# A second block of picked columns on TensorE in each octet of a graph layer

## The chip, the core and the metric

The kernel runs on one core of one Trainium2 chip. Its time is the device time of one execution; of three executions before the change the median is 3237.42 us (3233.37 to 3243.10). Times are in microseconds (us) unless another unit stands beside them. The engines are named as in the profile: PE is TensorE (PEld its weight loads), DVE is VectorE, ACT is ScalarE, POOL is GpSimd, and SP is SyncE, which here only issues transfers.

## The reference

One layer of a graph network over 12500 nodes with 64 features and 400000 edges, sorted by destination, all in float32:

```python
m_in = concatenate([x[src], x[dst], edge_attr])       # 64 + 64 + 16 features an edge
h = silu(m_in @ W1 + b1)                              # first layer, 64 wide
messages = silu(h @ W2 + b2)                          # second layer, 64 wide
agg = segment_sum(messages, dst, num_segments=12500)
y = silu(concatenate([x, agg]) @ W3 + b3)
out = layernorm(x + y)
```

The kernel's main difficulty is `x[src]`: the sources are random, so each of the 400000 edges wants a row (or, transposed, a column) of 64 floats from some place.

## The kernel before

The edges are cut into tiles of 128, and eight tiles are an **octet**; there are 391 octets, and one loop over `o` (the loop over `NO + 2`) writes out the work of all engines, software-pipelined: while octet `o` is in its first layer, octet `o - 2` is in its second and the messages of octet `o - 4` are added up. Two tiles that are computed side by side, one on the upper and one on the lower 64 partitions, are a **pair**; an octet has four.

What a source's node contributes to an edge can come to the first layer in several ways, and the work is split over them:

- GpSimd gathers a tile's 128 rows with one indirect DMA (`gather`, line 504). Early octets read the node features; from octet 12 on they read the table `pa`, which holds the features already multiplied by their part of W1. TensorE then transposes these rows (line 606).
- ScalarE copies single columns out of `xs` and `x2`, which hold all nodes' features transposed on chip; one activation serves two edges of a pair (`columns`, line 414). The column's address is a register, loaded in batches (line 397).
- VectorE does the same with a byte-wise maximum (line 416), also two edges at a time.
- SyncE issues one small DMA a row (`rows`, line 444).
- TensorE **picks** (`pick`, line 370): it loads the identity as weights and streams a single column of `xs`, so that the column lands in PSUM. A pick is one matmul in the code and two in the records. Sixteen addresses at a time are loaded into registers ahead of them (line 363).

A pair that one of the last four has filled is not gathered. Picked columns collect in the upper part of the two PSUM banks `pg`, whose lower part takes the sums of line 637. Odd octets use one bank, even ones the other. When both banks have a page of 128 columns, `place` lets VectorE copy it into `px` (line 381), and the first layer multiplies it like any other pair (line 609). `filled`, `whole`, `pairs`, `slots` and `counts` work out which octet takes a finished pair.

How much each of them does in an octet is set by constants: `ACOLS` (48 columns ahead of the first activation of an octet and 32 ahead of the second on ScalarE; in one octet of four it is 16 fewer), `VCOLS` with `VRATE` (32 columns at two or three places on VectorE), `PCOLS` (picks of TensorE), and `ROWS` (rows of SyncE, as a fraction).

On each engine the instructions run in the order in which the loop writes them; there is no scheduler for TensorE, ScalarE, VectorE and SyncE. In an octet TensorE's order is:

1. `turn` (line 571): transposes of the one-hot rows of the next octet, which VectorE then copies out (line 581); the buffer is single, so line 571 waits for that copy;
2. `window_product` (line 528);
3. `first_layer` (lines 606, 609, 610), whose result ScalarE activates at line 613;
4. `pick` (lines 363 and 370);
5. `add_up` (line 637);
6. `second_layer` (lines 622 and 624), whose result ScalarE activates at line 628; that buffer is single too, so line 622 waits for ScalarE;
7. in about half of the octets one product for the nodes' own layer: `node_x` (line 680) or `node_sums` (line 686).

## Time and profile before

| | before |
|---|---|
| median of 3 executions | 3237.42 us |
| profiled execution | 3241.3 us |
| its span, first to last instruction | 3239.4 us |
| mean granted TensorE clock | 0.836 |
| TensorE busy | 2713.9 us, 84% |
| ScalarE busy | 3076.0 us, 95% |
| VectorE busy | 2052.1 us, 63% |
| GpSimd busy | 2428.7 us, 75% |

Busy time leaves out the instructions that load registers and those that issue transfers; an engine can be occupied where this table calls it idle, and the idle time before a group ("issue" where nothing else is seen to hold it up) has to be read with it. The durations of matmuls overlap, so a group's busy time is not its count times its mean. The granted clock is TensorE's, as a share of full speed.

### The profile page before, as it was taken

To read this page: it belongs to the slowest core of one execution; us is meant where nothing else is said; L and a number is where in the kernel's file an instruction comes from. 1 tells how busy PE (TensorE), PEld (TensorE's weight loads), DVE (VectorE), ACT (ScalarE), POOL (GpSimd) and SP (SyncE) were. 2 spreads that over 40 slices of the span, in tenths; PEclk is the share of its full clock that TensorE was granted. 3 is DMA by queue.
4 is the path that set the end of the run, shared out by engine and by line. 5 is a ranking of instruction groups with operands and counts; after the bars stand their busy time and mean duration, and the time that the engine had idled before them with its cause. 6 is when DMAs were issued, how large, how long until landed. Compare 5 with 4: busy or idle time off the path is not lost. (4 is left out here: it accounts for less than half of the span.)

```text
span 3239.4 us, 111913 instructions
## 1 busy us (share of the span) xinstructions
PE 2713.9 (84%) x27140; PEld 2268.4 (70%) x27140; DVE 2052.1 (63%) x18157; ACT 3076.0 (95%) x15178; POOL 2428.7 (75%) x2567
## 2 busy tenths in 40 slices
PE   6888888889888888888888888888888888888865
PEld 4677767767777777776776776777776767777654
DVE  4466666666666666666666666666666666666663
ACT  1599999999999999999999999999999999999993
POOL 7777777777777777777777777777777777777775
PEclk7788888888788888788888888887888888788888
DMA  7222222222222222221222222222222222222121
GB/s 143 53 41 41 45 41 41 43 43 41 44 48 44 44 43 41 44 43 39 50 46 39 45 43 39 45 43 44 49 41 41 43 43 43 41 48 46 41 41 38
DMA packets 158957, 148.18 MB, mean 46 GB/s; under 512 B 102367, under 2 KB 112357, under 8 KB 157525
## 3 DMA queue, kind: packets, MB, share of 16 engines
q0 software_dynamic: 81888, 84.02, 14.6%
q1 hardware_dynamic: 61902, 47.16, 5.7%
q10 hardware_dynamic: 14502, 9.75, 1.4%
q8 instruction: 221, 3.62, 0.5%
q14 instruction: 444, 3.63, 0.4%
HBM read 134.30 MB, written 6.40 MB: 43 GB/s over the span
## 5 line engine op out<-in xcount | busy, mean ns | idle before, releaser
L504 POOL DMA_INDIRECT ga<-pa,sc x2463 | 2336.6, 949 | 756.8 <-issue 659.9
L414 ACT ACTIVATE cx<-xs,x 128x1 f32 x14336 | 2805.5, 382 | 9.8 <-issue 4.8
L416 DVE TENSOR_TENSOR cx<-xs,x 128x4 uint8 x15744 | 1271.9, 154 | 1043.4 <-issue 1027.3
L370 PEld LDWEIGHTS pg<-xs,ident 128*64 128x64 f32 x11776 | 770.6, 146 | 363.2 <-issue 310.3
L370 PE MATMUL pg<-xs,ident 128*64 x11776 | 801.6, 202 | 32.5 <-DVE px L381 31.8
L624 PEld LDWEIGHTS p<-w2d,h 128*128 128x128 f32 x3126 | 537.1, 243 | 244.4 <-issue 224.8
L624 PE MATMUL p<-w2d,h 128*128 128x128 f32 x3126 | 539.7, 330 | 0.0
L610 PE MATMUL p<-oh,xw 128*128 128x512 f32 (+1 forms) x758 | 454.6, 686 | 0.0
L622 PE MATMUL p<-b2r,one 128*128 128x512 bf16 x391 | 177.7, 454 | 229.3 <-ACT m L628 228.3
L571 PE MATMUL ph<-identb,eh 128*96 128x128 bf16 x1563 | 195.6, 261 | 169.3 <-DVE oh L581 165.5
L637 PE MATMUL pg<-eh,m 128*64 128x48 f32 x6250 | 320.4, 236 | 1.4 <-ACT m L628 1.4
L613 ACT ACTIVATE h<-p 128x512 f32<-128x512 f32 x391 | 263.4, 674 | 50.5 <-PE p L610 25.7
L628 ACT ACTIVATE m<-p 128x512 f32<-128x512 f32 x391 | 263.5, 674 | 36.2 <-PE p L624 34.5
L571 PEld LDWEIGHTS <-eh 128*96 128x96 bf16 x1563 | 153.9, 154 | 198.3 <-DVE oh L581 191.3
L606 PE MATMUL p<-ident,ga 128*128 128x128 f32 x1232 | 249.8, 319 | 45.8 <-DMA ga<-pa,sc 45.6
L637 PEld LDWEIGHTS pg<-eh,m 128*64 128x64 f32 x6250 | 269.9, 148 | 18.1 <-issue 15.1
L581 DVE COPY oh<-ph 96x512 f32<-96x512 f32 x391 | 263.1, 673 | 1.2 <-PE ph L571 1.2
L606 PEld LDWEIGHTS p<-ident,ga 128*128 128x128 f32 x1232 | 189.6, 171 | 54.7 <-issue 48.3
L553 DVE TENSOR_TENSOR eh<-wrow,dc 128x384 f32<-128x384 f32 x392 | 213.0, 544 | 17.8 <-ACT z L692 8.7
L528 PE MATMUL mm<-w1bb,xr 66*96 66x128 f32 x782 | 201.3, 347 | 8.4 <-DMA xr<-in_xt 8.3
L610 PEld LDWEIGHTS p<-oh,xw 128*128 128x128 f32 x758 | 139.3, 229 | 0.0
L528 PEld LDWEIGHTS mm<-w1bb,xr 66*96 66x96 f32 x782 | 127.1, 210 | 9.7 <-DMA xr<-in_xt 5.8
(115 smaller groups left out, 1194.0 us busy)
## 6 DMA issues: line engine op xcount, KB each, us to landing
rx<-pa SPq DMA_DIRECT2D x6400, 0.2 KB
ga<-pa,sc POOLq DMA_INDIRECT x2463
oh<-in_attr SPq DMA_DIRECT2D x130, 192.0 KB
xr<-in_xt SPq DMA_DIRECT2D x391, 24.4 KB
cxi<-in_src_pair SPq DMA_DIRECT2D x235, 1.0 KB
xs<-in_xt ACTq DMA_DIRECT2D x6, 512.0 KB
pa<-v ACTq DMA_DIRECT2D x12, 256.0 KB
x<-in_xt ACTq DMA_DIRECT2D x6, 512.0 KB
```

Of the source, the lines that this page charges most:

```text
L370: nc.tensor.matmul(g[:, s, k:k + 1], ident[:, :D], xs.bitcast(U8)[:, ds(at, 4)].bitcast(F32), start=True, stop=True, skip_group_check=True)
L414: nc.scalar.activation(cols[key][:, k:k + 1], word(i, xb, XADDR), AF.Identity, bias=word(i + 4, x2b, X2ADDR))
L416: nc.vector.tensor_tensor(t[:, 4 * k:4 * k + 4], at(i, xb, XADDR), at(i + 4, x2b, X2ADDR), op=OP.max)
L504: nc.gpsimd.indirect_dma_start(out=ga[:, i, :], out_offset=None, in_=x if o < RAW else pa[:, :], in_offset=bass.IndirectOffsetOnAxis(ap=sc ...
L528: nc.tensor.matmul(pw[:E, :], winrow[o], w1bb.rearrange("k s m -> k (s m)"), start=True, stop=True)
L571: nc.tensor.matmul(ph[:E, i, :], eh[:, i, :, 1], identb, start=(i == 0), stop=(i == k - 1), skip_group_check=True)
L606: nc.tensor.matmul(p1[:, i, :], g2.rearrange("p s d -> p (s d)"), ident, is_transpose=True, start=(i == c), stop=False, skip_group_check=True)
L610: nc.tensor.matmul(p1[:, :k], xw[o % 3], oh, start=False, stop=True, skip_group_check=True)
L613: nc.scalar.activation(h[:, :k], p1[:, :k], AF.Silu)
L624: nc.tensor.matmul(p2[:, 2 * i:2 * i + 2, :].rearrange("p s d -> p (s d)"), h[:, i, :], w2d, start=False, stop=(i == k - 1), skip_group_ch ...
L628: nc.scalar.activation(m[:, :n2], p2[:, :n2], AF.Silu)
L637: nc.tensor.matmul(pg[s * D:(s + 1) * D, :], m[:, i, :], eh[:, i // 2, :, s], start=(i < 2), stop=(i >= n - 2), skip_group_check=True)
```

## The change

Four constants change, and `pick` is called twice in an octet, each time for 16 columns: once where it stood, behind the first layer, and once behind the second layer (`behind()` writes `add_up` and `second_layer`), ahead of the product for the nodes. A page of 128 columns in each bank is then full after 8 octets instead of 16. ScalarE takes the smaller number of columns in one octet of three instead of one of four (74.7 columns an octet on average instead of 76), VectorE 81.6 instead of 83.2, SyncE 16.8 rows instead of 17.1; what is left goes to GpSimd's gathers, of which there are 36 fewer.

```diff
-PCOLS = 16
-ROWS = (256, 15)
-VRATE = (26, 10)
+PCOLS = 32
+ROWS = (1024, 61)
+VRATE = (51, 20)
...
             if eng == ENG.Activation:
-                return ACOLS if (o - BEGIN) % 4 < 3 else (ACOLS[0] - 16, ACOLS[1])
+                return ACOLS if (o - BEGIN) % 3 < 2 else (ACOLS[0] - 16, ACOLS[1])
...
-        def pick(o):
+        def pick(o, lo, up):
             if o < BEGIN:
                 return
-            c, hi, b = filled(o, o % 2), filled(o + 1, o % 2), o % 2
+            b = o % 2
+            c, hi = filled(o, b) + lo, filled(o, b) + up
             while c < hi:
...
                 if o < NO:
                     first_layer(o)
-                pick(o)
+                pick(o, 0, PCOLS // 2)
...
                 if o != NO - 1:
                     behind()
+                pick(o, PCOLS // 2, PCOLS)
                 for f, a in todo.get(o, []) if o < NO else []:
                     if f in (node_begin, node_x, node_sums):
                         f(*a)
```

`pick` is one line longer, so the lines behind its head stand one lower in the changed kernel (line 370 becomes 371, 637 becomes 638).

## The prediction

> **What bounds the kernel now.** I read the page's engine table and costliest groups first, then the waits, then the granted clock, and last TensorE's timeline beside the clock. Units are us; a group's columns are busy time, mean ns of one, and idle time before it.

> ```profile
> PE 2713.9 (84%) x27140; PEld 2268.4 (70%) x27140; DVE 2052.1 (63%) x18157; ACT 3076.0 (95%) x15178; POOL 2428.7 (75%) x2567
> ...
> L504 POOL DMA_INDIRECT ga<-pa,sc x2463 | 2336.6, 949 | 756.8 <-issue 659.9
> L414 ACT ACTIVATE cx<-xs,x 128x1 f32 x14336 | 2805.5, 382 | 9.8 <-issue 4.8
> L416 DVE TENSOR_TENSOR cx<-xs,x 128x4 uint8 x15744 | 1271.9, 154 | 1043.4 <-issue 1027.3
> L370 PE MATMUL pg<-xs,ident 128*64 x11776 | 801.6, 202 | 32.5 <-DVE px L381 31.8
> ```

> From the full list of groups, the gathers of the start:

> ```profile
> L504 POOL DMA_INDIRECT ga<-in_x,sc x96 | 91.2, 950 | 31.6 <-issue 27.1 <-DMA ga<-in_x,sc 2.3 <-DMA sc<-in_src_c 1.3
> ```

> GpSimd is the bound: 2336.6 busy plus 756.8 of gap, nearly all "issue", is 3093.4 for 2463 gathers, 1.256 each; with the 96 gathers of the start, 91.2 and 31.6, it fills 3216 of the 3239.4 span. ScalarE stands at 95%. VectorE's 2052 plus 1027 of register loading before its columns is 3079, also 95%. TensorE alone has room, 525 idle, and the waits say on whom:

> ```profile
> PE p L622 <- ACT m L628: 228.3, 167, 3.3
> PE ph L571 <- DVE oh L581: 165.5, 121, 5.3
> PE p L606 <- DMA ga<-pa,sc: 45.6, 36, 3.8
> PE pg L370 <- DVE px L381: 31.8, 17, 3.2
> ```

> It waits for VectorE and ScalarE far more than for gathers: it is early nearly everywhere. The granted clock of the run:

> ```profile
> core 0: 3239.4 us, clock 0.836
> ```

> ```profile
> 2402.82 0.66 PE L571 MATMUL ph<-identb,eh 128*96 128x128 bf16 x4 [1.59 <-DVE oh L581]
> ...
> 2406.45 3.47 PE L370 MATMUL pg<-xs,ident 128*64 x31
> 2409.68 0.34 PE L637 MATMUL pg<-eh,m 128*64 128x48 f32 x1
> ...
> 2413.00 0.63 PE L571 MATMUL ph<-identb,eh 128*96 128x128 bf16 x4
> ...
> 2416.12 1.97 PE L370 MATMUL pg<-xs,ident 128*64 x31
> 2417.90 0.26 PE L637 MATMUL pg<-eh,m 128*64 128x48 f32 x1
> ...
> 2419.70 0.39 PE L571 MATMUL ph<-identb,eh 128*96 128x128 bf16 x4
> ...
> 2421.68 1.97 PE L370 MATMUL pg<-xs,ident 128*64 x31
> ```

> A cold octet (half clock, no wait inside) takes 2413.00 - 2402.82 = 10.18, a warm one 2421.68 - 2416.12 = 5.56. Sixteen picks take 2417.90 - 2416.12 = 1.78 and one record more, say 1.85, warm, and 3.23 and one more, say 3.3, cold.

> What sets the clock? It changes only on a grid of 3.413. I laid that grid over the trace and asked for TensorE's busy time in each step, first of all lines (length, PE busy, weight loads, DVE, ACT, POOL, granted clock), then of the picks alone (length, PE busy, weight loads, clock):

> ```profile
> 807.90:811.31 3.41, 3.41 (x56) 3.20 (x56) 2.08 (x18) 3.41 (x19) 2.50 (x4) 1.00 0.32 78
> 811.31:814.72 3.41, 3.41 (x38) 2.65 (x36) 1.76 (x23) 3.41 (x18) 2.50 (x4) 1.00 0.23 43
> ...
> 828.38:831.79 3.41, 2.65 (x49) 2.50 (x49) 1.97 (x24) 3.41 (x19) 2.69 (x3) 1.00 0.19 37
> 831.79:835.20 3.41, 1.72 (x8) 1.62 (x8) 1.90 (x19) 3.41 (x19) 2.59 (x3) 0.50 0.50 126
> ```

> ```profile
> 807.90:811.31 3.41, 2.03 (x32) 1.94 (x32) 1.00 0.32 78
> ...
> 828.38:831.79 3.41, 2.03 (x32) 1.94 (x32) 1.00 0.19 37
> ```

> ```profile
> 2405.34:2408.75 3.41, 3.41 (x24) 2.30 (x22) 1.94 (x20) 3.41 (x19) 2.52 (x3) 0.50 0.20 37
> 2408.75:2412.16 3.41, 3.41 (x34) 3.23 (x35) 2.15 (x20) 3.41 (x19) 2.50 (x4) 0.50 0.13 25
> 2412.16:2415.58 3.42, 3.42 (x16) 2.93 (x16) 1.85 (x18) 3.15 (x17) 2.54 (x3) 0.50 0.19 32
> 2415.58:2418.99 3.41, 3.41 (x53) 2.79 (x52) 2.24 (x21) 3.41 (x20) 2.76 (x3) 1.00 0.37 94
> ```

> ```profile
> 2405.34:2408.75 3.41, 2.29 (x22) 2.30 (x22) 0.50 0.20 37
> 2408.75:2412.16 3.41, 1.28 (x12) 1.19 (x12) 0.50 0.13 25
> 2412.16:2415.58 3.42, 0.00 (x0) 0.00 (x0) 0.50 0.19 32
> ```

> Subtract the picks. Warm, the step with 3.41 - 2.03 = 1.38 of other matmuls stayed warm; the one with 2.65 - 2.03 = 0.62 was followed by half speed, though TensorE was busy for 78% of it. Cold, 3.41 - 2.29 = 1.12 and 3.41 - 1.28 = 2.13 of other matmuls stayed cold with TensorE busy throughout; 3.42 of them brought full speed back. So a pick, a matmul that streams one column, counts for next to nothing. **Staying warm needs other matmuls for a share between 18% and 40% of a step, getting warm again a share between 62% and 100%.** Counting over the whole trace only the time in which columns stream, the lines that part best lie at 0.38 (12 of 632 warm steps on the wrong side) and about three quarters (9 of 309 cold ones).

> **The change, part by part.** Off GpSimd: 36 gathers (2463 to 2427 at line 504, now 505) by 1.256 = 45. Off ScalarE: 256 activations (14336 to 14080) by 2805.5/14336 = 0.196 = 50. Off VectorE: 384 operations by (1271.9 + 1027.3)/15744 = 0.146 = 56, less what twice the pages ask of it, 96 more copies at 0.215 and 24 more address operations at 0.297, together 28, so 28 net:

> ```profile
> L381 DVE COPY px<-pg 64x64 f32<-64x64 f32 x92 | 19.7, 215 | 1.4
> L486 DVE TENSOR_SCALAR pxi<-pxi 1x256 int32<-1x256 int32 x23 | 6.8, 297 | 0.3
> ```

> Sync issues 256 fewer rows and 24 more index loads, less work in all. Each has less to do, so if nothing else happened the profiled 3241.3 (its span, and 1.9 around it) would become 3241.3 - 45 = 3196.

> On TensorE: 6144 columns more, in 376 octets that now hold two blocks of 16 instead of one. Warm that is 376 x 1.85 = 696, cold 376 x 3.3 = 1241. Each block also loads its 16 addresses into registers:

> ```profile
> PEld pg L370 <- issue: 310.3, 346, 1.5
> ```

> The new load lies under lines 623 and 625, which hide it as line 610 does now; where TensorE has just waited at 623 it may show, by at most these 310.3/346 = 0.9, and only where TensorE was early. I take nothing. The page's 2713.9 busy plus even 696 is 3410, over the 3196: it fits only if the other work runs warmer than now. Per octet with the matmuls for the nodes:

> ```profile
> L686 PE MATMUL wrow<-w3s,agg 128*128 128x64 f32 x192 | 53.9, 373 | 0.6 <-DVE eh L553 0.6
> L680 PE MATMUL wrow<-w3x,xs 128*128 128x64 f32 x192 | 53.7, 372 | 0.0
> ```

> those add 107.6/391 = 0.28. Warm: 5.56 + 0.28 + 1.85 = 7.7. Cold: 10.18 + 0.28 + 3.3 = 13.8. The picks run from 102.0 to 3083.1 in 368 octets, 8.10 each:

> ```profile
> L370 PE MATMUL pg<-xs,ident x11776: 188/197/268, 102.0 to 3083.1; 128*64 x200
> ```

> With h the share of time at half speed, TensorE completes (1 - h)/7.7 + h/13.8 octets per us, and keeps up with 8.0 per octet (8.10 less 45/376) only for h under 0.09, a granted clock over 0.95.

> Where the new block stands decides h. TensorE, an octet without node products, from its first layer on; before:

> ```order
> L610 MATMUL p_121171<-oh,xw_178 128x512
> L363 TENSOR_LOAD pxi
> L370 MATMUL pg_238<-xs,ident 64x1 x16
> L637 MATMUL pg_238<-eh,m 64x48 x8
> L622 LDWEIGHTS one_120
> L622 MATMUL p_121404<-b2r,one_120 128x512
> L624 MATMUL p_121404<-w2d,h 128x128 x4
> L571 LDWEIGHTS eh
> ```

> and now (line numbers one higher):

> ```order
> L611 MATMUL p_112481<-oh,xw_170 128x512
> L364 TENSOR_LOAD pxi
> L371 MATMUL pg_237<-xs,ident 64x1 x16
> L638 MATMUL pg_237<-eh,m 64x48 x8
> L623 LDWEIGHTS one_120
> L623 MATMUL p_112752<-b2r,one_120 128x512
> L625 MATMUL p_112752<-w2d,h 128x128 x4
> L364 TENSOR_LOAD pxi
> L371 MATMUL pg_237<-xs,ident 64x1 x16
> L572 LDWEIGHTS eh
> ```

> The unbroken run from line 637 over 571 to 610 is cut in two. In an octet with a node product, TensorE's second block is followed by it:

> ```order
> L623 MATMUL p_118788<-b2r,one_120 128x512
> L625 MATMUL p_118788<-w2d,h 128x128 x4
> L364 TENSOR_LOAD pxi
> L371 MATMUL pg_237<-xs,ident 64x1 x16
> L687 MATMUL wrow<-w3s,agg 128x64
> L572 LDWEIGHTS eh
> ```

> Before, that product stood among other matmuls; now it lengthens a block that hardly streams.

> *Cold.* Now a run of 10.18 - 3.3 = 6.9 of counting work stands between blocks, so some step lies wholly inside it. After: 3.3 (lines 638 to 625, 2409.73 to 2413.00) and 3.6 (572 to 611, 2402.82 to 2406.45) between blocks of 3.3. A step of 3.41 holds three quarters, 2.55, of a run at 3.3 + 3.41 - 5.1 = 1.6 of its 3.41 offsets, or at 1.9 for the longer run. The runs start 6.6 apart, 1.94 steps, and the octet of 13.8 is 4.04 steps: the same offset comes back, and one that misses goes on missing. I take 0.57 to warm within the octet, after 0.6 of one on average; the other 0.43 drift by some 0.2 per octet through a band of 1.5, on average 3.6 octets. Mean cold stay: 0.57 x 0.6 + 0.43 x 4.1 = 2.1 octets.

> *Warm.* A step that holds a whole block keeps 40%, just over 0.38. A node product of some 0.4, mostly weight load, or any wait of over 0.1 beside a block takes it under. About 190 of 391 octets have such a product, and I put such a step at 4 in 10 of them; the waits at lines 622 and 571, and those for page copies, of which there are now twice as many, stand beside blocks too. I take 3 octets for a warm stay, with 2 and 9 as ends.

> Sum: (3 x 7.7 + 2.1 x 13.8)/5.1 = 10.2 per octet. 102 before the first pick + 376 x 10.2 + the tail of 3239.4 - 3083.1 less 8 octets of 8.1 = 92 + 1.9 around the span = **4030**. The other engines' 45 to 56 then vanish in waiting for TensorE. Ends: 9 warm to 1.4 cold give 8.5 and 3390; 2 warm to 4 cold give 11.8 and 4630; its own range is 3600 to 4500. The profiled run lies 0.1% over the median of 3237.42.

> **The rivals.** *TensorE gets warmer and GpSimd stays the bound: 3196, faster.* For it: 525 idle is filled, and idle is what sends the clock down now. Against it: a step busy for 78% fell, and picks fill idle time without counting. It decides at a clock of 0.95. [...]

> *The share of half speed stays 33%:* 1/(0.67/7.7 + 0.33/13.8) = 9.0, so 102 + 376 x 9.0 + 92 + 2 = 3580, slower. New blocks lose warmth and filled waits gain it; nothing in the rows makes them cancel exactly.

> *TensorE hardly ever gets warm again:* 13.8 throughout, 102 + 376 x 13.8 + 94 = 5385. The offset that comes back speaks for it; the 0.2 to 0.4 by which node products and the number of transposes shift an octet, against it.

> **How the numbers follow.** Forecast, 3600 to 4500: 0.62. The share unchanged or somewhat lower, 3260 to 3600: 0.18. GpSimd's bound: 0.12. Hardly ever warm: 0.05. Nothing to tell: 0.03. A difference under 0.3% is about what a measurement of this kernel can tell from none (its runs spread by that). So faster 0.12, same 0.03, slower 0.85. For 8 in 10 the range reaches down into the second case and leaves out the fast one and the top: 3260 to 4500.

> **What would show it.** Right: a granted clock well under 0.836, TensorE near 100% busy, the waits at lines 623 and 572 gone, ScalarE and VectorE waiting for lines 611 and 625, GpSimd for its buffers; steps filled by blocks and one run stay at 0.50. Wrong: a clock over 0.95, or warm steps whose other matmuls fill under a third. If only the price is off, the stays of 3 and 2.1 octets are what to measure.

## The result, and the profile after

The change makes the kernel slower by 45%: 4712.66 us median of 4 executions (4671.9 to 4767.75) against 3236.94 (3233.37 to 3243.1), ratio 1.4509 with a 95% interval of 1.4402 to 1.4616. The profiled execution took 4746.7, 0.7% over its median. The ratio is one of means: it leaves out the two executions of the change that lie over 1.5% above its fastest (4746.7, the profiled one, and 4767.75) and counts two that are not in the median (4731.97 and 4707.12). All times are us.

From the page of the changed kernel, the engine table, the first gathers, and the picks; then its waits and its clock:

```profile
PE 4693.4 (99%) x39447; PEld 3987.6 (84%) x39447; DVE 2077.6 (44%) x17887; ACT 3165.0 (67%) x14922; POOL 2389.0 (50%) x2531
...
L505 POOL DMA_INDIRECT ga<-pa,sc x2427 | 2297.2, 947 | 2301.5 <-PE p L607 1549.9
...
L371 PE MATMUL pg<-xs,ident 128*64 x24064 | 2267.5, 228 | 0.4 <-issue 0.4
```

```profile
POOL ga L505 <- PE p L607: 1549.9, 300, 12.5
...
DVE agg L649 <- PE pg L371: 1019.5, 238, 14.0
...
ACT m L629 <- PE p L625: 573.5, 244, 2.8
ACT h L614 <- PE p L611: 568.0, 263, 4.1
```

```profile
core 0: 4744.9 us, clock 0.614
```

The roles are exchanged. TensorE is busy 99% of the time and hardly waits for anybody (40 in all); GpSimd, which waited 6.4 for that line before, stands 1550 for gather buffers that line 607 has not emptied; ScalarE waits 1142 for the two layers; VectorE waits 1020 before it takes the sums of line 638, until TensorE has made the picks behind them, which go into the same bank (in the stretch below it takes them at 1613.20, behind the second block, though the matmuls of line 638 ended by 1609.99). TensorE's mean clock fell from 0.836 to 0.614: half speed for 77% of the time instead of 33%. The rest of the change does not show: 2427 gathers still cost 0.947 each.

How the clock falls is seen in one stretch without a node product, cut on the grid of 3.413 on which the record of the clock changes (every stay in the records of before and of the change is a whole number of such steps). First TensorE's timeline, then the steps with all lines (length, PE busy, ..., granted clock), then the picks alone:

```profile
1607.31 2.12 PE L371 MATMUL pg<-xs,ident 128*64 x31
1609.24 0.26 PE L638 MATMUL pg<-eh,m 128*64 128x48 f32 x1
...
1610.15 1.05 PE L625 MATMUL p<-w2d,h 128*128 128x128 f32 x8
1611.13 2.03 PE L371 MATMUL pg<-xs,ident 128*64 x32
1613.09 0.43 PE L572 MATMUL ph<-identb,eh 128*96 128x128 bf16 x4
...
1615.43 3.47 PE L371 MATMUL pg<-xs,ident 128*64 x31
...
1622.11 3.57 PE L371 MATMUL pg<-xs,ident 128*64 x32
1625.61 0.66 PE L572 MATMUL ph<-identb,eh 128*96 128x128 bf16 x4
...
1629.24 2.93 PE L371 MATMUL pg<-xs,ident 128*64 x26
```

```profile
1604.26:1607.68 3.42, 3.42 (x13) 1.92 (x12) 2.06 (x18) 0.20 (x1) 2.41 (x3) 0.50 0.12 20
1607.68:1611.09 3.41, 3.41 (x56) 3.25 (x55) 1.57 (x18) 2.88 (x15) 2.50 (x4) 1.00 0.33 88
1611.09:1614.50 3.41, 3.41 (x46) 3.09 (x44) 0.67 (x2) 3.13 (x17) 2.66 (x3) 1.00 0.17 30
1614.50:1617.92 3.42, 3.42 (x26) 2.50 (x24) 2.08 (x18) 3.42 (x18) 2.65 (x3) 0.50 0.21 36
1617.92:1621.33 3.41, 3.41 (x33) 3.23 (x33) 1.29 (x17) 2.52 (x14) 2.50 (x4) 0.50 0.18 33
1621.33:1624.74 3.41, 3.41 (x29) 3.19 (x29) 2.36 (x20) 1.94 (x9) 0.52 (x1) 0.50 0.09 17
```

```profile
1604.26:1607.68 3.42, 0.37 (x4) 0.37 (x4) 0.50 0.12 20
1607.68:1611.09 3.41, 1.80 (x31) 1.72 (x30) 1.00 0.33 88
1611.09:1614.50 3.41, 2.03 (x32) 1.94 (x32) 1.00 0.17 30
1614.50:1617.92 3.42, 2.49 (x24) 2.50 (x24) 0.50 0.21 36
1617.92:1621.33 3.41, 1.08 (x11) 0.99 (x10) 0.50 0.18 33
1621.33:1624.74 3.41, 2.63 (x25) 2.63 (x26) 0.50 0.09 17
```

TensorE is busy in every step, and the clock still changes. The step from 1604.26 holds the run of lines 607 to 611 and only 0.37 of picks: the clock gets warm. The next holds the first block and the run behind it and stays warm. The third, at 1611.09, holds the whole second block, all 32 records: the clock is cold from 1614.50 on. From there blocks and runs alternate so that no step holds enough of one run: 1617.92 has 1.08 of picks, and half speed stays. Columns stream for 0.85 of the step that warms the clock, for 0.46 and 0.38 of the two warm ones, and for 0.71 of the one from 1617.92. This is an estimate from spacings in the same trace: records of 512 float32 columns (line 611) start 853 ns apart at half speed, 1.67 a column, and 432 at full speed, where half of 1.67 is taken; bf16 columns (line 572, 128 in 107 and 56) count half of that, picks nothing.

Over the trace, from 200 to 4600, I read the lengths of all stays off the clock's record. 94 of 117 warm stays last two steps and 23 four, mean 2.39 (8.2). The cold ones last 5 steps (54 of them), 9 (25), 17 (11), 1 (11), 21 (7), 13 (6) or 25 (3), mean 8.49 (29.0): every one is one step and a multiple of four. The cold octet above is 1629.24 - 1615.43 = 13.81, 4.05 steps; the 116 octets that ran wholly at half speed took 13.81 to 14.78, 14.07 on average, so each met the grid 0.2 to 1.1 later than the last one, 0.4 on average.

### The profile page after: what moved, and what is told of

It reads as the page before. It is cut to its first block, busy times and chain, and to the rows that moved or that the text cites. A ratio compares the mean times of both kernels' runs of the same rounds, so it can differ in the third digit from the quotient of the medians.

```text
span 4744.9 us, 135795 instructions
## 1 busy us (share of the span) xinstructions
PE 4693.4 (99%) x39447; PEld 3987.6 (84%) x39447; DVE 2077.6 (44%) x17887; ACT 3165.0 (67%) x14922; POOL 2389.0 (50%) x2531
## 4 chain that ended last, share of the span: by engine, by line
PE 98%; DMA 1%; DVE 1%; ACT 0%; issue 0%; ACTq 0%; SPq 0%; DVEq 0%
PE pg L371 46%; PE p L611 13%; PE p L625 11%; PE pg L638 7%; PE p L607 5%; PE p L623 4%; PE ph L572 3%; PE mm L529 3%; PE p L610 2%; PE wrow L687 1%; PE wrow L681 1%; PE mm L217 1%; PE p L602 0%; PE p L594 0%; DMA xr<-in_xt 0%; DMA oh<-in_attr 0%
## 5 line engine op out<-in xcount | busy, mean ns | idle before, releaser
L415 ACT ACTIVATE cx<-xs,x 128x1 f32 x14080 | 2697.4, 280 | 318.8 <-issue 303.6
L371 PEld LDWEIGHTS pg<-xs,ident 128*64 128x64 f32 x24064 | 2203.5, 194 | 612.9 <-issue 579.8
L371 PE MATMUL pg<-xs,ident 128*64 x24064 | 2267.5, 228 | 0.4 <-issue 0.4
L649 DVE TENSOR_TENSOR agg<-agg,pg 128x48 f32 x391 | 79.6, 204 | 1415.8 <-PE pg L371 1019.5
L611 PE MATMUL p<-oh,xw 128*128 128x512 f32 (+1 forms) x758 | 687.7, 1009 | 0.0
L625 PEld LDWEIGHTS p<-w2d,h 128*128 128x128 f32 x3126 | 618.7, 276 | 26.6 <-issue 1.3
L625 PE MATMUL p<-w2d,h 128*128 128x128 f32 x3126 | 615.0, 363 | 0.0
L638 PE MATMUL pg<-eh,m 128*64 128x48 f32 x6250 | 415.5, 275 | 1.4 <-ACT m L629 1.4
L638 PEld LDWEIGHTS pg<-eh,m 128*64 128x64 f32 x6250 | 358.6, 185 | 9.0 <-issue 6.1
L572 PE MATMUL ph<-identb,eh 128*96 128x128 bf16 x1563 | 215.9, 279 | 3.8 <-DVE eh L554 3.0
L623 PE MATMUL p<-b2r,one 128*128 128x512 bf16 x391 | 203.5, 521 | 1.2 <-ACT m L629 1.2
L611 PEld LDWEIGHTS p<-oh,xw 128*128 128x128 f32 x758 | 188.8, 305 | 0.0
L572 PEld LDWEIGHTS <-eh 128*96 128x96 bf16 x1563 | 157.0, 165 | 8.8 <-DVE eh L554 4.2
```

The source lines that it names most:

```text
L371: nc.tensor.matmul(g[:, s, k:k + 1], ident[:, :D], xs.bitcast(U8)[:, ds(at, 4)].bitcast(F32), start=True, stop=True, skip_group_check=True)
L415: nc.scalar.activation(cols[key][:, k:k + 1], word(i, xb, XADDR), AF.Identity, bias=word(i + 4, x2b, X2ADDR))
L572: nc.tensor.matmul(ph[:E, i, :], eh[:, i, :, 1], identb, start=(i == 0), stop=(i == k - 1), skip_group_check=True)
L611: nc.tensor.matmul(p1[:, :k], xw[o % 3], oh, start=False, stop=True, skip_group_check=True)
L623: nc.tensor.matmul(p2[:, :n2, :], one3, b2r[:, :n2, :], start=True, stop=False, skip_group_check=True)
L625: nc.tensor.matmul(p2[:, 2 * i:2 * i + 2, :].rearrange("p s d -> p (s d)"), h[:, i, :], w2d, start=False, stop=(i == k - 1), skip_group_ch ...
```

## The experiments

All kernels of one comparison ran beside the kernel before, which took 3233 to 3238. Seven more runs, six of kernels that are in the table and one with 16 and 8 columns, fell on chips on which the kernel before itself took 5324 to 5328; they stand at the end of this section and carry no reading. The table holds the runs; where no number of runs is given with them, it was one execution. "Stays" are mean lengths in steps of 3.413 from the clock's record of each trace, from 200 to 100 before its end.

| run | what | time | clock | warm stay | cold stay |
|---|---|---|---|---|---|
| before | 16 | 3237 | 0.836 | 4.1 | 1.9 |
| the change | 16 and 16 | 4713 | 0.614 | 2.4 | 8.5 |
| e1_picks16 | 16, rest as changed | 3258 | 0.830 | 4.4 | 2.2 |
| e2_wide | 16 and 16 wide matmuls | 3299 | 0.965 | 29.2 | 1.2 |
| e3_block32 | 32 in one block | 3848 | 0.769 | 1.8 | 1.6 |
| e4_bias4 | the change, bias four times | 4160 | 0.791 | 2.9 | 2.1 |
| f1_16_12 | 16 and 12 | 4130 | 0.686 | 8.7 | 15.5 |
| f2_node_first | node product ahead | 4731 | 0.614 | 2.5 | 9.0 |
| f3_12_12 | 12 and 12 | 3647 | 0.757 | 2.9 | 2.8 |
| f4_before_12_12 | before, 12 and 12 | 3636 | 0.763 | 3.3 | 2.9 |
| h1_dup4 | the change, four picks made twice | 4390 | 0.724 | 2.0 | 2.5 |
| h2_before_one24 | before, 24 in one block | 3274 | 0.849 | 3.5 | 1.5 |
| h3_before_one20 | before, 20 in one block | 3235 | 0.825 | 2.6 | 1.4 |

### Is it the picks, and is it the clock?

My theory: one-column matmuls do not count for the clock, the second block keeps it down, and TensorE at half speed is what takes the time. Two rivals: the other engines' new shares cost it; or TensorE is overloaded by the number of added matmuls, whatever the clock does.

The picks alone undone:

```diff
-PCOLS = 32
+PCOLS = 16
...
-                pick(o, 0, PCOLS // 2)
+                pick(o, 0, PCOLS)
...
-                pick(o, PCOLS // 2, PCOLS)
```

> The picks alone undone: 16 columns an octet in one block behind the first layer, ScalarE, VectorE and SyncE as in the change; 2571 gathers instead of 2523 in the change and 2559 before. Theory (the second block of picks keeps TensorE's clock down): GpSimd is the bound again, 3241 + 12 x 1.256 = 3256, clock 0.80 to 0.87. Rival (something else in the change, the other engines' new shares, costs the time): over 4000. Output unchanged.

Measured 3257.68, a clock of 0.830. That is 25 over the kernel before that ran beside it (3232.82), of which the 12 gathers were to make 15; the other engines' new shares do not cost the 1476 of the change.

The second block made of matmuls that stream 64 columns (the second call says `wide=True`; `spare` is the other page of the bank, which is set to zero at the start):

```diff
+                    if wide:
+                        nc.tensor.matmul(spare[:, i % 2 * D:(i % 2 + 1) * D], ident[:, :D], xs[:, i * D:(i + 1) * D],
+                                         start=True, stop=True, skip_group_check=True)
+                        continue
```

> The second block keeps its 16 addresses, its 32 matmul records and the identity as weights, but each streams 64 columns of the node features into a spare page instead of one picked column. It leaves out the second half of the picks, so the pages that VectorE copies hold other numbers there. Theory (a one-column matmul does not count for the clock): clock over 0.95, waits at lines 623 and 572 back, about 3200 to 3270. Rival (TensorE is overloaded by the number of added matmuls, whatever they stream): same count, same weight loads, so 4600 or more.

Measured 3299.05. Engine table, one of GpSimd's waits (its lines are numbered a little higher), and clock of this run:

```profile
PE 3177.9 (96%) x39447; PEld 2748.5 (83%) x39447; DVE 2050.5 (62%) x17889; ACT 3053.1 (93%) x14922; POOL 2396.1 (73%) x2531
```

```profile
POOL ga L512 <- PE p L614: 79.9, 54, 5.8
```

```profile
core 0: 3297.3 us, clock 0.965
```

The same 39447 records as in the change, and 1414 less. The wide records start 58 ns apart at full speed, as the picks do, so the block itself has not become shorter. So it isn't the number of matmuls. The wide matmuls differ from picks in one more thing: their addresses are fixed and do not come from registers; no run takes the two apart. The time is also 30 more than I expected at most, and over the kernel before: TensorE stands at 96% at nearly full speed, and GpSimd waits 79.9 for buffers of the first layer, against 6.4 before; of the waits at lines 623 and 572, 25 at 572 is all that came back. Even at a clock of 0.965 this load on TensorE does not pay; what a clock that never fell would give, no run shows.

All 32 columns in one block:

```diff
-                pick(o, 0, PCOLS // 2)
+                pick(o, 0, PCOLS)
...
-                pick(o, PCOLS // 2, PCOLS)
```

> All 32 columns in one block behind the first layer, none behind the second; same work on every engine. Theory (what matters is how much other work fits unbroken into a step of 3.41): lines 638 to 611 are one run of 6.9 again at half speed, so every octet holds a step that warms the clock; a block of 3.7 fills a step, so every octet also cools it. Cold stays of 1 to 3 steps instead of 8.5, half speed for 40 to 50% of the time, 9.5 an octet, about 3770 (3600 to 4000). Rival (overload by the added matmuls' own time): the same matmuls, so 4600 to 4800.

Measured 3847.59 at a clock of 0.769: the same matmuls, 865 less than the change. Cold stays are of 1 or 2 steps, 1.6 on average, half speed takes 46% of the time. All 362 octets between 200 and 3726 run in part at each speed: the block cools the clock, and the whole run behind it warms it again. Span times clock, an estimate of the time that the run would take at full speed throughout, is 2957 here and 2913 in the change, so the 865 are the clock's.

More work on TensorE, in the right place:

```diff
-            nc.tensor.matmul(p2[:, :n2, :], one3, b2r[:, :n2, :], start=True, stop=False, skip_group_check=True)
+            for _ in range(4):
+                nc.tensor.matmul(p2[:, :n2, :], one3, b2r[:, :n2, :], start=True, stop=False, skip_group_check=True)
```

> The change with the bias matmul of line 623 (512 columns, 0.23 warm, 0.40 cold) issued four times in a row, each overwriting the same sums with the same values: more work on TensorE. Theory: the run behind the first block grows from 3.3 to 4.5 at half speed, so a step of 3.41 finds three quarters of itself in it at most offsets, and the octet of 15.2 is no longer a whole number of steps: cold stays shorten from 8.5 to about 4 steps, 11 an octet, about 4270 (3900 to 4550), faster than the change for all its extra work. Rival (overload): 376 x (0.78 x 1.2 + 0.22 x 0.68) = 410 more than the 4712 of the change, about 5120.

Measured 4160.31:

```profile
PE 4099.5 (99%) x40620; PEld 3331.0 (80%) x40620; DVE 2067.9 (50%) x17887; ACT 3148.8 (76%) x14922; POOL 2388.9 (57%) x2531
```

```profile
core 0: 4158.5 us, clock 0.791
```

1173 records more than the change, and 552 less: three useless matmuls an octet pay. They stream (512 columns each, 0.23 at full speed in the stretch above, 1609.92 to 1610.15), and they also make the octet longer, which shortens the cold stays by itself (h1_dup4 below); this run does not part the two. Both rivals have fallen.

### What ends the warm stay?

I had predicted warm stays of three octets; they last one. Either the second block with its ends takes the step after a warming under the line by itself (A), or the node product behind it does (B).

```diff
-                pick(o, PCOLS // 2, PCOLS)
                 for f, a in todo.get(o, []) if o < NO else []:
                     if f in (node_begin, node_x, node_sums):
                         f(*a)
+                pick(o, PCOLS // 2, PCOLS)
```

> The change with the node product (lines 676, 681, 687) ahead of the second block instead of behind it. Same work, output unchanged. Theory A (the block and its ends alone take the step after a warming under 0.38): about the same, 4500 to 4750. Theory B (it is the node product joined to the block that takes it under): the product now borders on line 625 and separates nothing more from the block, octets without a product hold the clock, so the clock is over 0.68 and the time 4000 to 4350.

Measured 4731.37 at 0.614, stays of 2.5 and 9.0 steps: the time is A's, and B's forecast is out. That the product does not matter is not shown, though. In the change, the second step of a warm stay, which holds 28 to 32 of the second block's 32 records, was followed by half speed in all 75 stays in which it also held a part of a node product, and in 19 of the 42 in which it held none. Here the product still lies in that step in 41 stays, and all 41 end there; of the 68 others that reach a second step 38 do. The block alone takes that step under the line about every other time, the block with a product every time.

```diff
-PCOLS = 32
+PCOLS = 28
...
-                pick(o, 0, PCOLS // 2)
+                pick(o, 0, 16)
...
-                pick(o, PCOLS // 2, PCOLS)
+                pick(o, 16, PCOLS)
```

> The change with 28 columns an octet, 16 behind the first and 12 behind the second layer; GpSimd gathers 2535 instead of 2523. Output unchanged. Theory (the step that follows a warming holds the whole second block and falls under 0.38): the block hardly streams for 24 records x 0.058 + 0.2 at its ends = 1.6 instead of 2.0, so that step keeps (3.41 - 1.6) x 0.93/3.41 = 0.49, or 0.40 with a node product: it now stays warm, warm stays grow from 2.4 steps to 5 or more, and the clock rises over 0.75. About 3500 (3250 to 3800). Rival (TensorE's time goes with the number of picks): 4 of 32 columns less, 376 x 4 x 0.19 = 280 under the 4712 of the change, 4430.

Measured 4130.0 at 0.686, neither my 3500 nor the rival's 4430. The warm stays grew as expected, from 2.4 to 8.7 steps. The time did not follow, since the cold stays nearly doubled, to 15.5 steps, some of them over 40. Of the 145 octets that ran wholly at half speed, the 90 with a node product take 13.45 to 14.10, the middle one 13.67: four steps are 13.653. The 55 without one take 12.94 to 13.60, the middle one 13.15. My expectation had taken the cold stay as given; it seems to belong to the octet's length, which the next run tests.

### What makes a cold stay long?

If it is the octet's length as a multiple of the step, then lengthening the octet by picks alone must shorten the stays.

```diff
-        def pick(o, lo, up):
+        def pick(o, lo, up, again=0):
...
-                for i in range(n):
+                for i in list(range(again)) + list(range(n)):
...
-                pick(o, PCOLS // 2, PCOLS)
+                pick(o, PCOLS // 2, PCOLS, again=4)
```

> The change with the first four picks of every second block made twice (the same columns into the same places): 8 more one-column records an octet, 0.47 warm and 0.85 cold, and nothing else. Output unchanged. Theory (a cold stay lasts because the cold octet of 13.8 to 14.3 is four steps of 3.41 and a little, so that each octet meets the steps at nearly the same offset): the octet becomes 14.9, 4.36 steps, the offset moves by a third of a step each time, and stays of 9, 13 and 17 steps vanish: mean under 6 steps instead of 8.5, and the added time is mostly won back, 4500 to 4800. Rival (a cold stay ends by chance, so longer blocks make it longer): mean 8.5 or more, and 4712 + 376 x (0.78 x 0.85 + 0.22 x 0.47) = 5000 or more.

Measured 4390.43, even under the range that I expected:

```profile
PE 4337.0 (99%) x42450; PEld 3652.2 (83%) x42455; DVE 2074.1 (47%) x17887; ACT 3161.3 (72%) x14922; POOL 2388.0 (54%) x2531
```

```profile
core 0: 4388.6 us, clock 0.724
```

3003 records more of the very kind that does not count, and 322 less than the change. Of its 261 cold stays between 200 and 4200, 165 last one step, 95 five and one nine; no longer ones are left. That a cold stay's length hangs on the octet's length, and not on chance, is shown. The offset did not wander as I had expected, though: every warm stay lasts two steps, two warm steps and a cold one are three, and the octets that mix both speeds take 10.2 in the middle, 2.99 steps. The loop has fallen into another, cheaper repetition.

### Fewer picks, cut or whole

> The change with 24 columns an octet, 12 behind each layer; 2547 gathers. Output unchanged. Theory: neither block alone takes a step under 0.38, and the margin of the first block, 0.40 before, grows to 0.5: GpSimd nearly the bound at 3241 - 12 x 1.256 = 3226, so 3230 to 3330 at a clock over 0.85. At half speed both runs are still cut, by blocks of 2.5, so a cold stay is longer than before: if that decides, 3400 to 3700. Rival (load by number of picks): 376 x 8 x 0.19 = 570 under 4712, 4140.

(The change with `PCOLS = 24`.) Measured 3647.24 at 0.757. The number of picks as a load would have given 4140; but the clock isn't held as I had hoped either. Its cold stays are mostly of 2 or 4 steps, where one block has 1 or 2: "if that decides" is the half of the expectation that came true. What the other half left out is in the trace, in the step from 1671.46 and the one behind it, and in the timeline of the first:

```profile
1671.46:1674.87 3.41, 3.41 (x39) 3.21 (x39) 1.78 (x18) 2.62 (x12) 0.53 (x2) 1.00 0.07 15
1674.87:1678.29 3.42, 3.42 (x23) 2.16 (x21) 2.08 (x18) 3.42 (x18) 2.75 (x3) 0.50 0.15 27
```

```profile
1671.55 1.56 PE L371 MATMUL pg<-xs,ident 128*64 x24
1673.04 0.68 PE L687 MATMUL wrow<-w3s,agg 128*128 128x64 f32 x2
```

Of the 122 warm steps between 200 and 3545 that hold 24 records of picks or more and a part of a node product, 117 were followed by half speed; of the 284 with as many picks and no product, 12 were. Here it is mostly the product beside the block that ends a warm stay.

The kernel before with 12 and 12, and with the same 24 in one block:

```diff
-PCOLS = 16
+PCOLS = 24
...
-                pick(o)
+                pick(o, 0, PCOLS // 2)
...
+                pick(o, PCOLS // 2, PCOLS)
```

> The kernel before with 24 columns an octet, 12 behind each layer, and ScalarE, VectorE and SyncE as before: 2535 gathers instead of 2559. Output unchanged. Theory: blocks of 12 leave every warm step over 0.38 unless something waits beside them; if the clock keeps its 0.836, TensorE completes 0.67/7.25 + 0.33/12.9 = 0.118 octets per us, 8.5 an octet, too slow for GpSimd's 8.02: 3370; if it rises to 0.90, 3237 - 24 x 1.256 = 3207. I expect the clock to rise, since the first block's step goes from 0.40 to 0.5: 3207 to 3290. Rival (load by number of picks): TensorE's 525 idle holds 376 x 8 x 0.12 = 360, so 3207.

Measured 3635.5 (4 runs), ratio 1.1242 (1.1188 to 1.1295). The clock fell to 0.763 instead of rising: I was wrong, and for the same reason. Of the 114 warm steps with 24 records of picks or more and a part of a node product 105 were followed by half speed, of the 305 without a product 15. In these two kernels, with 12 and 12, the line at 0.38 also misplaces 117 of 503 and 102 of 512 warm steps, and the best line is 0.43; what it is in a node product that does not count, no run shows.

> The kernel before with 24 columns an octet in one block behind the first layer, the other engines' shares as before: the same picks and the same 2535 gathers as with 12 and 12, which took 3635. Output unchanged. Theory (the cut of the run at half speed is what costs): lines 637 to 610 are one run again, cold stays 1 to 3 steps as with one block of 32, half speed for about 0.4 of the time; 0.6/6.8 + 0.4/12.2 = 0.121 octets per us, 8.3 an octet, just short of GpSimd's 7.95: about 3300 (3207 to 3400). Rival (the number of picks decides): 3635 again.

Measured 3273.81 (4 runs; the edit is `PCOLS = 24` alone), ratio 1.0118 (1.0102 to 1.0134), clock 0.849. The same picks and the same 2535 gathers cost 362 less in one block than in two. Span times clock is 2767 with two blocks and 2778 with one: the work at full speed is the same, and the difference is the clock's. Cutting the run is what costs, not the number of picks.

> The kernel before with 20 columns an octet in one block, other shares as before, 2547 gathers. Output unchanged. Theory: half speed for up to 0.4 of the time still lets TensorE complete 0.6/6.3 + 0.4/11.3 = 0.131 octets per us, 7.7 an octet, under GpSimd's 7.99: GpSimd stays the bound, 3237 - 12 x 1.256 = 3222, 0.995 of before. Rival (TensorE has no room left): over 3250.

Measured 3234.72 (11 runs; the edit is `PCOLS = 20` alone), ratio 0.9997 (0.9988 to 1.0006): no difference. TensorE has room for 20, as the theory says, but the 12 gathers saved bring nothing at the median, though GpSimd is occupied 14 less. With ScalarE at 95%,

```profile
PE 2913.0 (90%) x30213; PEld 2503.4 (78%) x30218; DVE 2059.2 (64%) x18187; ACT 3077.2 (95%) x15178; POOL 2413.8 (75%) x2555
```

it may be ScalarE's turn to bound; no run here took work off it and left the rest, so this stays open. No version beat the kernel before.

### Seven runs on slower chips

Beside a kernel before of 5328.04, these took 6432.67 (16 and 12), 6154.94 (16 and 8: the second call of the first edit above ends at column 24), 5779.49 (12 and 12) and 6691.47 (node product ahead):

> The change with 28 columns an octet, 16 behind the first and 12 behind the second layer; GpSimd gathers 2535 instead of 2523. Output unchanged. Theory (the step that follows a warming holds the whole second block and falls under 0.38): the block hardly streams for 24 records x 0.058 + 0.2 at its ends = 1.6 instead of 2.0, so that step keeps (3.41 - 1.6) x 0.93/3.41 = 0.49, or 0.40 with a node product: it now stays warm, warm stays grow from 2.4 steps to 5 or more, and the clock rises over 0.75. About 3500 (3250 to 3800). Rival (TensorE's time goes with the number of picks): 4 of 32 columns less, 376 x 4 x 0.19 = 280 under the 4712 of the change, 4430.

> The change with 24 columns an octet, 16 behind the first and 8 behind the second layer; 2547 gathers. Output unchanged. Theory: a block of 8 hardly streams for 1.1, no step falls under 0.38 by it, and at half speed it is short (1.7): clock over 0.82, GpSimd nearly the bound at 3241 - 12 x 1.256 = 3226, so 3230 to 3350. Rival (load by number of picks): 376 x 8 x 0.19 = 570 under 4712, 4140.

> The change with 24 columns an octet, 12 behind each layer; 2547 gathers. Output unchanged. Theory: as many picks as with 16 and 8, but neither block alone takes a step under 0.38, and the margin of the first block, 0.40 before, grows to 0.5: clock as high or higher than with 16 and 8, 3230 to 3330. At half speed both runs are cut by blocks of 2.5, so a cold stay is longer: if that decides, 3400 to 3700. Rival (load by number of picks): 4140, and the same as 16 and 8.

> The change with the node product (lines 676, 681, 687) ahead of the second block instead of behind it. Same work. Theory A (the block and its ends alone take the step after a warming under 0.38): about the same, 4500 to 4750. Theory B (it is the node product joined to the block that takes it under): the product now borders on line 625 and separates nothing more from the block, octets without a product hold the clock, so the clock is over 0.68 and the time 4000 to 4350.

and beside a kernel before of 5323.83, these took 7061.66 (four picks twice), 5675.09 (24 in one block) and 5578.22 (20 in one block):

> The change with the first four picks of every second block made twice (the same columns into the same places): 8 more one-column records an octet, 0.47 warm and 0.85 cold, and nothing else. Output unchanged. Theory (a cold stay lasts because the cold octet of 13.8 to 14.3 is four steps of 3.41 and a little, so that each octet meets the steps at nearly the same offset): the octet becomes 14.9, 4.36 steps, the offset moves by a third of a step each time, and stays of 9, 13 and 17 steps vanish: mean under 6 steps instead of 8.5, and the added time is mostly won back, 4500 to 4800. Rival (a cold stay ends by chance, so longer blocks make it longer): mean 8.5 or more, and 4712 + 376 x (0.78 x 0.85 + 0.22 x 0.47) = 5000 or more.

> The kernel before with 24 columns an octet in one block behind the first layer, the other engines' shares as before: the same picks and the same 2535 gathers as with 12 and 12, which took 3635. Output unchanged. Theory (the cut of the run at half speed is what costs): lines 637 to 610 are one run again, cold stays 1 to 3 steps as with one block of 32, half speed for about 0.4 of the time; 0.6/6.8 + 0.4/12.2 = 0.121 octets per us, 8.3 an octet, just short of GpSimd's 7.95: about 3300 (3207 to 3400). Rival (the number of picks decides): 3635 again.

> The kernel before with 20 columns an octet in one block, other shares as before, 2547 gathers. Output unchanged. Theory: half speed for up to 0.4 of the time still lets TensorE complete 0.6/6.3 + 0.4/11.3 = 0.131 octets per us, 7.7 an octet, under GpSimd's 7.99: GpSimd stays the bound, 3237 - 12 x 1.256 = 3222, 0.995 of before. Rival (TensorE has no room left): over 3250.

In the waits of the run with the node product ahead, TensorE stops between matmuls of one line, for nothing that the profile shows:

```profile
PE pg L638 <- issue: 876.1, 908, 1.9
```

All seven traces have such waits of TensorE, 1119 to 1832 in all; in the traces of the table they come to 2.5 at most. What makes them is not known. Time in which TensorE stands idle is also time in which no column streams, so these times answer none of the questions; the same kernels ran again above, but for 16 and 8, which is left without a result.

## Why the prediction was right and where it failed

The direction and the mechanism were right: TensorE becomes the bound, its clock falls well under 0.836, the waits at lines 623 and 572 go (1.2 and 3.8 are left of 229 and 169), GpSimd waits for buffers. The size was wrong: 4030 forecast, 4713 measured, over the range's 4500, and over the 4630 that the prediction had worked out for its own worst end.

- **GpSimd bounds before:** in part. With the picks undone and 12 gathers more, the time was 3258 against 3256 worked out (e1_picks16); but 12 gathers less gained nothing (h3_before_one20), so GpSimd is not the only bound.
- **A pick does not count for the clock:** right: with 64 columns streamed in the place of each of the second block's picks the clock was 0.965 instead of 0.614 (e2_wide). With columns that stream counted alone, the line at 0.38 puts 9 of 311 warm steps of the changed kernel on the wrong side, and 3 of 892 in e2_wide. For cold steps the best line in the changed kernel is 0.715. Both are nearly one line if it is counted in columns: records of 128 float32 columns start 109 to 112 ns apart at full speed and 213 at half, so 0.38 of a warm step and 0.715 to 0.75 of a cold one both hold about 1500 columns of such records (an estimate from these spacings). With 12 and 12 the line of 0.38 fails beside node products.
- **Prices of an octet:** nearly right. Warm 7.53 to 7.76 without a node product and 8.06 to 8.28 with one (7.7 was forecast for the mean). Cold 13.81 to 14.45 without and 14.31 to 14.78 with one, 14.1 on average (13.8 forecast), since a second block takes 1625.61 - 1622.11 = 3.50 cold, not 3.3: the last record of line 625 before it and the first of line 572 behind it each stand off a little more (0.351 and 0.175 between starts, where records of lines 625 and 371 follow their own kind at 0.213 and 0.107).
- **The mean cold stay:** right, 29.0 and so 2.1 octets of 14, and the reason, an offset that nearly returns, was right too. That the mean came out exactly is luck: the short stays (of 1 or 5 steps, 65 of the 117) last 1.05 octets and not 0.6, the long ones 3.3 and not 4.1, and the two errors cancel.
- **The warm stay of 3 octets is the step that failed.** I put a fall at 4 in 10 of the octets with a node product, as if a block met the grid at a random offset. It doesn't: in all 117 stays the step that warms the clock lies on the run of lines 572 to 611, so the next one holds the first block and the one after it the second, 28 to 32 of its 32 records. That step was followed by half speed in all 75 stays with a part of a node product in it, and in 19 of the 42 without; the other 23 ended two steps later. Measured: 8.2, 1.1 octets. With 1.1 in the place of 3 the forecast's own sum gives (1.1 x 7.7 + 2.1 x 13.8)/3.2 = 11.7 an octet and 102 + 376 x 11.7 + 94 = 4595, inside 3% of what was measured; with the cold octet's 14.1 as well it gives 4670.
- **The rivals.** That TensorE gets warmer fell: TensorE was busy 99% of the time at a clock of 0.614. The rival's price of 3196 was too low as well: e2_wide, with wide matmuls for the second block's picks, had a clock over its 0.95 and took 3299. The unchanged share of half speed (3580) fell. Hardly ever warm (5385) was as far off as the forecast, 14% on each side, at a chance of 0.05: the range's upper end gave it too little.

## What to carry to other kernels

TensorE's busy share does not tell its clock: here 99% went with 0.614, and 96% with 0.965. Lay the clock's grid of steps (3.413 in these traces) over the timeline and count the time in which columns stream. In this kernel it paid to put work that hardly streams in one block rather than in two (3848 against 4713, 3274 against 3636), so that the matmuls that do stream form runs that fill a step at half speed; look also whether the period of the loop at half speed is near a whole number of steps. Where the loop met the grid right after a warming was not random here: follow the two steps behind it instead of giving them a chance.

## What the runs showed that I had not expected

- Time came off by adding work: three more bias matmuls an octet took 552 off the change, four more repeated picks 322.
- The cold stays are quantised: in the change they last 1, 5, 9, 13, 17, 21 or 25 steps and nothing between, since a cold octet of 13.81 to 14.78 is four steps of 3.413 and a little.
- Two warm steps with the same busy time and the same picks (3.41 busy, 2.03 of picks at 807.90 before and at 1611.09 after) can be followed by different clocks. Columns stream for 0.38 to 0.39 of both, so they lie on the line and counting columns does not part them; what decides there stays open.
